# Three fp32r products of split halves in place of seven fp32 block products

## The chip, the cores and the metric

The kernel runs on one core of a Trainium2 chip. A core has five engines with an instruction stream each: TensorE (PE, matrix products; its weight loads are listed as PEld), VectorE (DVE), ScalarE (ACT), GpSimd (POOL) and SyncE (SP), which here issues every DMA. Each engine takes its instructions strictly in the order of its stream and waits where an operand isn't ready. SBUF is the working memory of 128 partitions; PSUM has eight banks into which PE writes its products. The metric is the device time in microseconds (us); lower is better. This text numbers the batch elements from 0 to 31 and calls the work of one turn of the outer loop a batch.

## The reference

The input x has 32 elements of 512 rows and 512 columns; adj is a 512 x 512 matrix of zeros and ones. Two layers follow each other, both with a residual and a layer normalisation:

```python
q, k, v = x @ Wq + bq, x @ Wk + bk, x @ Wv + bv        # 8 heads of 64 columns
scores = einsum('bihd,bjhd->bhij', q, k) / 8 + where(adj == 0, -1e9, 0)
x = layernorm(x + softmax(scores) @ v)
y = einsum('nm,bmd->bnd', adj, x)                      # aggregation
x = layernorm(x + y @ weight + bias)                   # convolution
```

The four products with a weight (three projections and the convolution) are 512 x 512 x 512 each, for every element.

## The kernel before

`fast_kernel` writes out the order of the work by hand; no scheduler moves an instruction. The tiles of one name and tag form a ring of a fixed number of buffers: a new tile takes the oldest buffer and waits until its last reader is done. All products go through one ring of eight PSUM banks.

Each of the four weight products is made by seven block products of 256 x 256 x 256 instead of eight (`FACTORS`, `block_product`, L365), in fp32, with sums of blocks of the weight made once (`sum_weights`) and sums of blocks of the transposed x (`combine_rows`, `sum_rows` on POOL) made for every element. The results are combined while they are taken out of the banks (`project`, L385 to L402, and `convolve`, L533 to L556). The weights stay in SBUF for the whole run.

The main loop runs over the elements b and two groups g of four heads. For a group, in this order:

- `attend` (L604, PE): exponentials times values, for two pairs of heads. `fold_squares` (L641, L643, DVE) and a DMA of parts sum the exponentials over the keys; `turn_out` (L621, DVE) transposes a pair's output and sends it to DRAM, from where `fetch_rows` (L629) brings it back as rows. `fetch_parts` (L655) brings the parts back.
- `scores` of the next group (L580, PE), sixteen banks, which DVE empties with the mask added (L582) and ACT exponentiates (L584). POOL adds the exponentials of the key blocks (`add_exponentials`, L595).
- for g = 0, `load_squares` of element b + 2 (L253): sixteen DMAs of 64 KB, in squares of 32, into the ring `xin` of four.
- the units of the slot (`units_of`). The first slot has the products for q and k and two for v of element b + 1, and between them the statistics and normalisations of b - 2 and b - 1 and `turn_over` (store of b - 2, then the load of x of element b into the same buffer). The second slot has the rest of v, the aggregation of b - 1 with adj (`aggregate`, L487, in fp32r, from a high and a low half of x that `split` makes: L455 on ACT, L459 on DVE), the four 32 x 32 transposes of element b + 2 (`turn_squares`, L350), and the convolution of b - 1, with the transposes between its products.

`scale_rows` (L675, ACT) and `add_rows` (L679, POOL) bring the attention's output into the residual. At the two ends of the run the order is written out separately: the first element is transposed on PE (`x_transpose`), and the last element's aggregation is done by rows (`aggregate_rows`) with the last normalisation in halves.

Of the kernel before, what the change touches and what calls it, by code (L numbers as in the profile page):

```python
# [23 lines left out]
FACTORS = {1: ("A11", "B11"), 2: ("A12", "B21"), 3: ("S4", "B22"), 4: ("A22", "T4"),  # L53
           5: ("S1", "T1"), 6: ("S2", "T2"), 7: ("S3", "T3")}
ORDER = (1, 5, 6, 7, 2, 3, 4)

A_AT = {"A11": 0, "A12": 1, "A21": 2, "S3": 2, "A22": 3, "S1": 4, "S2": 5, "S4": 6}
B_AT = {"B11": 0, "B21": 1, "B12": 2, "T3": 2, "B22": 3, "T1": 4, "T2": 5, "T4": 6}
# [147 lines left out]

@with_exitstack
def fast_kernel(ctx: ExitStack, tc, verdict, x, adj, Wq, bq, Wk, bk, Wv, bv, W1, b1, out):
# [6 lines left out]
    assert N == 512 and D == 512 and H * HD == D and B > 2  # L215
# [12 lines left out]


    X, IN = {}, {}  # L230
    half = N // 2

    def load(b):
        X[b] = work.tile([P, NB, D], FP, name="xT" if b == B - 1 > 1 else "xs", bufs=1 if b == B - 1 > 1 else 2)
        nc.sync.dma_start(X[b], x[b].rearrange("(c p) d -> p c d", p=P))

    def load_block(b, c, cols=slice(0, D)):

        if (b, c) not in IN:
            IN[b, c] = work.tile([P, D], FP, name="xin", bufs=XIN)  # L240
        nc.sync.dma_start(IN[b, c][:, cols], x[b, c * P:(c + 1) * P, cols])  # L241

    def load_squares(b):


        for d in range(DB):
            IN[b, d] = work.tile([P, N // SQ, SQ], FP, name="xin", bufs=XIN)
            place_squares(IN[b, d], x[b], d)
# [6 lines left out]
    def load_factors(w, name, t=None):  # L255
        if t is None:
            t = consts.tile([P, 7, 2, half], FP, name=name)
        for s in range(2):
            nc.sync.dma_start(t[:, 2 * s:2 * s + 2, :, :].rearrange("p a c f -> p (a c) f"),
                              w[:, s * half:(s + 1) * half].rearrange("(c p) f -> p c f", p=P))  # L260
        return t


    wq = consts.tile([P, 7, 2, half], FP, name="wq")

    def load_factor(name, r, c):
        nc.sync.dma_start(wq[:, B_AT[name], :, :], Wq[r * half:(r + 1) * half, c * half:(c + 1) * half].rearrange(
            "(c p) f -> p c f", p=P))

    for c in range(2):  # L270
        load_block(0, c, slice(0, half))
    load_factor("B11", 0, 0)
    for c in range(2):
        load_block(0, c, slice(half, D))
    for c in (2, 3):
        load_block(0, c)
    for name, r, c in (("B21", 1, 0), ("B12", 0, 1), ("B22", 1, 1)):
        load_factor(name, r, c)
# [11 lines left out]

# [11 lines left out]
    def look_for_low_half(c):  # L302

        kept = work.tile([P, N], FR, name="high")
# [3 lines left out]
        nc.vector.tensor_tensor(cut, squares, kept.bitcast(FP), op=ALU.not_equal)  # L308
        nc.vector.tensor_reduce(inexact[:, c:c + 1], cut, axis=AX.X, op=ALU.add)

# [3 lines left out]
    def sum_weights(w, n):  # L314

        b11, b21, b12, b22, t1, t2, t4 = (w[:, i, :, :] for i in range(7))
        nc.vector.tensor_sub(*((t1, b12, b11), (b12, b22, b12), (t2, b22, t1), (t4, b21, t2))[n])

    def combine(w, bias, which=range(4)):

        for n in which:
            sum_weights(w, n)
        width = bias.shape[1] // 2
        nc.vector.tensor_sub(bias[:, width:], bias[:, width:], bias[:, :width])

    def combine_rows(t, engine=nc.gpsimd, which=range(3)):

        a11, a12, a21, _, s1, s2, s4 = (t[:, i, :, :] for i in range(7))
        for n in which:
            engine.tensor_sub(*((s2, s1, a11), (a21, a11, a21), (s4, a12, s2))[n])  # L330

    def x_transpose(b, c, sides=(0, 1)):
# [636 lines left out]
```

## Time and profile before

| what | value |
|---|---|
| median of three runs | 2728.31 us (2727.42 to 2728.68) |
| span of the profiled execution | 2726.6 us; the page gives no other time of this execution |
| mean granted clock of TensorE | 0.999 |
| instructions | 36269 |
| DMA | 179.16 MB, mean 66 GB/s |

In the profile, busy time is the time in which an engine has at least one instruction running. A group of instructions is one source line (L365 is line 365 of the kernel), one engine and one shape, with how many there were, how long one took and what its engine had waited for. In a timeline each row has a start (in us from the start of the span), a length and a count of merged instructions; what stands in brackets is the idle time before it and its releaser. An fp32 product of TensorE stands in the records as two matmul instructions, an fp32r product as one. SPq is SyncE's queue of DMA issues; "to landing" is the time from an issue until the data are there.

### The profile page before, as it was taken

The page shows a single profiled execution, that of the slowest core. Times are in us where ns is not written, and L with a number is a line of the kernel's source. Part 1 is how long each engine was busy: PE and PEld are TensorE (multiplying, and loading weights), DVE is VectorE, ACT ScalarE, POOL GpSimd, SP SyncE. Part 2 cuts the span into 40 slices and gives each one's busy share as a digit, 9 for nine tenths or more (in the row PEclk, how much of TensorE's full clock was granted, in tenths as well). Part 3 has the DMA queues.
Part 4 walks back from the last instruction along what each step waited for, and adds up shares of the span by engine and source line. Part 5 has one row for each costly group of instructions (what it writes and reads, how often), then busy time and mean ns, then how long its engine had stood idle before and what let it go on. Part 6 is the DMA issues. An engine that isn't in the chain of part 4 may idle for free.

```text
span 2726.6 us, 36269 instructions
## 1 busy us (share of the span) xinstructions
PE 2715.0 (100%) x12328; PEld 1899.7 (70%) x12328; DVE 2106.5 (77%) x3476; ACT 1411.2 (52%) x2462; POOL 1916.0 (70%) x1221
## 2 busy tenths in 40 slices
PE   9999999999999999999999999999999999999998
PEld 6676676766767767667676676776767767667666
DVE  7878777777777787877878778777787777877778
ACT  3455464554544655446555465554554545546455
POOL 4776677766867668676676776777767776667776
PEclk9999999999999999999999999999999999999999
DMA  6213231233222332223322233221232212323121
GB/s 162 49 34 80 70 73 36 60 80 74 69 41 60 76 77 66 46 56 75 80 63 50 55 71 80 63 65 45 67 80 67 63 44 65 80 71 73 34 76 53
DMA packets 641166, 179.16 MB, mean 66 GB/s; under 512 B 586960, under 2 KB 591568, under 8 KB 640976
## 3 DMA queue, kind: packets, MB, share of 16 engines
q1 hardware_dynamic: 640976, 176.79, 27.6%
q8 instruction: 99, 1.62, 0.2%
q14 instruction: 91, 0.75, 0.1%
HBM read 108.01 MB, written 68.68 MB: 65 GB/s over the span
## 4 chain that ended last, share of the span: by engine, by line
PE 99%; DVE 0%; DMA 0%; POOL 0%; SPq 0%; ACT 0%; issue 0%; ACTq 0%
PE bank L365 57%; PE bank L580 17%; PE bank L604 16%; PE bank L487 9%; PE bank L519 0%; DMA xin<-in_x_dram 0%; DVE xT L550 0%; POOL xT L547 0%; DVE part L903 0%; SPq L241 0%; DVE shift L439 0%; PE bank L685 0%; ACT xT L444 0%; DVE stat L906 0%; PE bank L339 0%
## 5 line engine op out<-in xcount | busy, mean ns | idle before, releaser
L584 ACT ACTIVATE e<-e 128x1024 f32<-128x1024 f32 x512 | 524.5, 1052 | 570.4 <-DVE e L582 535.6
L595 POOL TENSOR_TENSOR es<-e 128x1024 f32<-128x1024 f32 x128 | 315.7, 2466 | 480.1 <-ACT e L584 480.1
L582 DVE SCALAR_TENSOR_TENSOR e<-gap,bank 128x512 f32<-128x512 uint8 x1024 | 618.0, 682 | 20.2 <-PE bank L580 20.2
L595 POOL TENSOR_TENSOR es<-es,e 128x1024 f32<-128x1024 f32 x256 | 618.6, 2417 | 20.1
L580 PE MATMUL bank<-q,k 64*128 64x512 f32 x2048 | 463.4, 598 | 0.0
L604 PE MATMUL bank<-e,v 128*64 128x512 f32 x2048 | 453.6, 595 | 0.0
L365 PE MATMUL bank<-wv,xT 128*128 128x256 f32 x1792 | 405.4, 381 | 0.0
L365 PE MATMUL bank<-xT,wk 128*128 128x256 f32 x1792 | 402.4, 379 | 0.0
L365 PE MATMUL bank<-xT,wq 128*128 128x256 f32 x1792 | 400.9, 381 | 0.6 <-ACT xT L341 0.5
L365 PE MATMUL bank<-w,yT 128*128 128x256 f32 x1792 | 392.3, 379 | 0.0
L365 PEld LDWEIGHTS bank<-wv,xT 128*128 128x128 f32 x1792 | 337.6, 190 | 70.1 <-DVE e L582 24.3
L365 PEld LDWEIGHTS bank<-xT,wq 128*128 128x128 f32 x1792 | 337.6, 190 | 69.2 <-DVE e L582 23.5
L580 PEld LDWEIGHTS bank<-q,k 64*128 64x128 f32 x2048 | 203.8, 186 | 258.1 <-issue 159.7
L365 PEld LDWEIGHTS bank<-w,yT 128*128 128x128 f32 x1792 | 340.0, 190 | 48.1 <-DVE e L582 0.8
L365 PEld LDWEIGHTS bank<-xT,wk 128*128 128x128 f32 x1792 | 340.5, 190 | 46.3
L675 ACT ACTIVATE rows<-rows,zero,inverse 128x64 f32<-128x64 f32 x1008 | 343.3, 429 | 1.9 <-DVE inverse L662 1.9
L604 PEld LDWEIGHTS bank<-e,v 128*64 128x64 f32 x2048 | 141.4, 137 | 277.1 <-issue 275.4
L584 ACT ACT_TABLE_LOAD x30 | 38.5, 1283 | 412.1 <-DVE e L582 412.1
L459 DVE TENSOR_TENSOR low<-xs,high 128x512 fp32r<-128x512 f32 x122 | 160.7, 1317 | 92.1 <-ACT high L455 92.1
L550 DVE TENSOR_TENSOR xs<-bank,xs 128x512 f32<-128x512 f32 x186 | 124.4, 683 | 96.2 <-PE bank L365 56.7
L444 ACT ACTIVATE xs<-xs,shift,rstd 128x512 f32<-128x512 f32 x248 | 181.8, 803 | 27.4 <-DVE shift L439 18.2
L490 ACT ACTIVATE yT<-bank 128x512 f32<-128x512 f32 x124 | 74.1, 598 | 185.0 <-PE bank L487 185.0
(122 smaller groups left out, 3050.8 us busy)
## 6 DMA issues: line engine op xcount, KB each, us to landing
turned<-attT SPq DMA_DIRECT2D x126, 256.0 KB, 2.1
rows<-turned SPq DMA_DIRECT2D x504, 64.0 KB, 2.5
xin<-in_x_dram SPq DMA_DIRECT2D x496, 64.0 KB, 2.4
xs<-in_x_dram SPq DMA_DIRECT2D x31, 1024.0 KB, 5.3
out_dram<-xs SPq DMA_DIRECT2D x31, 1024.0 KB, 4.4
part<-passed SPq DMA_DIRECT2D x256, 8.0 KB, 1.8
passed<-part SPq DMA_DIRECT2D x64, 32.0 KB, 1.5
wq<-in_L_gnn_Wq_dram SPq DMA_DIRECT2D x4, 256.0 KB, 5.9
```

Source lines behind the costliest of these rows:

```text
L365: nc.tensor.matmul(pm[:, r, :], left[:, d, r * P:(r + 1) * P], right[:, d, :], start=(d == 0), stop=(d == 1))
L444: nc.scalar.activation(row, row, AF.Identity, bias=SHIFT[t][:, slot:slot + 1], scale=RSTD[t][:, slot:slot + 1])
L459: nc.vector.tensor_sub(LOW[b, d], cols, HIGH[b, d].bitcast(FP))
L487: nc.tensor.matmul(pm.rearrange("p a n -> p (a n)"), part, adjT[:, n % NB, :], start=(n == 0), stop=(n == 2 * NB - 1))
L490: nc.scalar.activation(yt[:, d // 2:d // 2 + 3:2, d % 2, :], pm, AF.Copy)
L550: nc.vector.tensor_add(block, pm, block)
L580: nc.tensor.matmul(ps[s], keys[:, j * P:(j + 1) * P], queries, start=True, stop=True)
L582: nc.vector.scalar_tensor_tensor(e[:, s, :], gap[:, j, :], NEG * root, ps[s], op0=ALU.mult, op1=ALU.add)
L584: nc.scalar.activation(e, e, AF.Exp, scale=1.0 / root)
L595: nc.gpsimd.tensor_add(ES[b, hp], ES[b, hp] if j > 1 else E[b, hp, 0], E[b, hp, j])
L604: nc.tensor.matmul(po[s * HD:(s + 1) * HD, :], values, e[:, s, :], start=(j == 0), stop=(j == NB - 1))
L675: nc.scalar.activation(part, part, AF.Identity, bias=zero, scale=inverse[:, c, s:s + 1])
```

## The change

Every operand of the four weight products is split into two fp32r parts, and a product is made by three fp32r passes over 512 columns, in rows of 128: high x high, rest x rest (both scaled so that they add into one bank, `near`) and a mixed product (`both` x `both`) in a second bank, `far`. Two instructions take the pair out: ACT and DVE for q and k, DVE twice for v and for the convolution. A transposed x, and the aggregated y, is kept as three planes (`HIGH`, `REST`, `BOTH`) in one tile `factors` with a single buffer, which x of an element and y of another use in turn. The split of a plane is an ACT copy with a scale, a DVE operation on it and its source, and a POOL subtraction.

The planes of Wv and of the last weight stay in SBUF. Those of Wq and Wk don't: the first element makes them in eight chunks of 128 columns and stores them in DRAM, and every later element fetches them again, three chunks ahead, through SyncE's queue (24 DMAs of 256 KB for an element).

The order of units is new. The first slot holds the eight products for q and k, the second slot those for v, the aggregation, then the scores of the next element (`take_scores`), the convolution and, after all of it, the transposes and splits of x (`flips`). The low half for the aggregation moves from DVE to POOL. The launch and the end of the run are rewritten for the new products: the first weights are split as they arrive, and the last element's convolution is normalised and stored row block by row block.

```diff
-FACTORS = {1: ("A11", "B11"), 2: ("A12", "B21"), 3: ("S4", "B22"), 4: ("A22", "T4"),
-           5: ("S1", "T1"), 6: ("S2", "T2"), 7: ("S3", "T3")}
+EPSILON = 2.0 ** -12
+SHRINK = 1.0 - 2.0 ** -13
...
+    def split_high(high, a):
+        nc.scalar.activation(high, a, AF.Copy, scale=EPSILON * SHRINK)
+    def split_rest(rest, high, a):
+        nc.vector.scalar_tensor_tensor(rest, plain(high), -1.0 / EPSILON, a, op0=ALU.mult, op1=ALU.add)
+    def split_both(both, high, rest, engine=nc.gpsimd):
+        engine.tensor_sub(both, plain(high), plain(rest))
+    def split_weight(high, rest, both, w, temp):
+        nc.scalar.activation(high, w, AF.Copy, scale=SHRINK / EPSILON)
+        nc.scalar.activation(temp, w, AF.Copy, scale=SHRINK)
+        nc.vector.scalar_tensor_tensor(rest, w, 1.0 / EPSILON, plain(high), op0=ALU.mult, op1=ALU.subtract)
+        nc.gpsimd.tensor_sub(both, plain(rest), plain(temp))
+    def factors(name="factors"):
+        return work.tile([P, 3, DB, N], FR, name=name, tag="factors", bufs=1)
...
+    def turn_squares(b, d):
+        TURN[b, d] = work.tile([P, N], FP, name="turn", bufs=2)
+        nc.vector.transpose(TURN[b, d], IN[b, d].rearrange("p j f -> p (j f)"))
+    def split_x(b, d):
+        if d == 0:
+            XT[b] = factors()
+        high, rest, both = (XT[b][:, f, d, :] for f in range(3))
+        a = TURN.pop((b, d))
+        split_high(high, a)
+        split_rest(rest, high, a)
+        split_both(both, high, rest)
+    def flips(b):
+        return [(turn_squares, b, 0), (turn_squares, b, 1), (split_x, b, 0), (turn_squares, b, 2), (split_x, b, 1),
+                (turn_squares, b, 3), (split_x, b, 2), (split_x, b, 3)]
...
+    SEQUENCE = [(which, m) for m in range(DB) for which in "qk"]
+    AHEAD = 3
+    def chunks():
+        return [work.tile([P, DB, P], FR, name="stream", bufs=3 * AHEAD) for _ in range(3)]
+    def fetch_chunk(n):
+        b, (which, m) = n // len(SEQUENCE), SEQUENCE[n % len(SEQUENCE)]
+        CHUNK[b, which, m] = chunks()
+        for f, part in enumerate(CHUNK[b, which, m]):
+            nc.sync.dma_start(plain(part), KEPT[which, m, f])
+    def three_passes(near, far, left, right):
+        for f, pm in ((HIGH, near), (REST, near), (BOTH, far)):
+            for d in range(DB):
+                nc.tensor.matmul(pm, left(f, d), right(f, d), start=(f != REST and d == 0),
+                                 stop=(f != HIGH and d == DB - 1))
+    def project(b, which, m):
...
+        three_passes(near, far, lambda f, d: w[f][:, d, :], lambda f, d: xt[:, f, d, :])
+        if n + AHEAD >= len(SEQUENCE):
+            fetch_chunk(n + AHEAD)
+        t = store[b, m] = work.tile([P, N], FP, name=which, bufs=DB)
+        nc.scalar.activation(t, near, AF.Identity, bias=bias[:, m:m + 1], scale=1.0 + EPSILON)
+        nc.vector.tensor_add(t, far, t)
...
+    def convolve(b, r):
+        near, far = bank(N), bank(N)
+        three_passes(near, far, lambda f, d: yt[:, f, d, r * P:(r + 1) * P], lambda f, d: w1[:, f, d, :])
+        nc.vector.scalar_tensor_tensor(row, near, 1.0 + EPSILON, row, op0=ALU.mult, op1=ALU.add)
+        nc.vector.tensor_add(row, far, row)
...
+    def first_slot(b):
...
+        ready = [(turn_over, b)]
...
+            behind = [seen[:2], seen[2:] + old[:2], old[2:] + fresh[:2], ready + fresh[2:], young[:2], young[2:]]
+        behind += [scaled + added]
+        return [(add_up, b, 0)] + merge(projections(b + 1), behind)
+    def second_slot(b):
...
+        units = merge(values(b + 1), [splits[:1], splits[1:2], splits[2:3], splits[3:]])
+        units += [(add_up, b, 1)] + gathered[:2] + scaled[:1] + gathered[2:] + [(take_scores, b + 1, 0)]
...
+        units += merge(convolved, [scaled[1:] + added[:1], added[1:]])
+        return units + flips(b + 2)
...
+                if b + 2 < B:
+                    load_squares(b + 2)
+                units = first_slot(b)
+                run(units[:2])
+                run(later)
+                run(units[2:])
```

## The prediction

> **What bounds the kernel now.** I read the page's engine row first, then the chain of work in order of time over one batch (from 1302.53 us), then the timelines of VectorE and of SyncE's queue at that place, and last the rows in which something was late.
>
> ```profile
> PE 2715.0 (100%) x12328; PEld 1899.7 (70%) x12328; DVE 2106.5 (77%) x3476; ACT 1411.2 (52%) x2462; POOL 1916.0 (70%) x1221
> ```
> ```profile
> 1302.53 7.02 PE bank L604 x32
> 1309.55 7.14 PE bank L580 x32
> 1316.69 27.82 PE bank L365 x128
> ...
> 1364.05 3.74 PE bank L487 x16
> ...
> 1387.06 7.02 PE bank L604 x32
> ```
> TensorE (PE) never stands still, and a batch takes 1387.06 - 1302.53 = 84.53 us. An fp32 product is two passes in the records: 27.82 / 128 x 2 = 0.435 us for 256 columns. An fp32r pass over 512 columns is 3.74 / 16 = 0.234.
>
> ```profile
> 1310.64 9.66 DVE L582 SCALAR_TENSOR_TENSOR e<-gap,bank 128x512 f32<-128x512 uint8 x16 [0.33 <-PE bank L580]
> ```
> VectorE ends its folds and turnings with the two `attend`s (the last turning at 1310.31) and begins to empty the score banks 1.09 us after the scores began. Here is what happens when it is late, from the start of the run (VectorE and PE):
> ```profile
> 117.87 2.48 DVE L350 STREAM_TRANSPOSE xT<-xin 128x512 f32<-128x512 f32 x4
> 126.40 9.62 DVE L582 SCALAR_TENSOR_TENSOR e<-gap,bank 128x512 f32<-128x512 uint8 x16
> 124.10 8.31 PE L580 MATMUL bank<-q,k 64*128 64x512 f32 x32
> ```
> Four transposes stand straight before the folds, the emptying begins 2.30 us after the scores began, and the scores take 8.31 us where the steady batches' same row has 7.21.
>
> SyncE's queue in the same batch:
> ```profile
> 1309.84 2.61 SPq L629 DMA_DIRECT2D rows<-turned  x4
> 1312.55 1.99 SPq L655 DMA_DIRECT2D part<-passed  x4
> 1314.64 0.38 SPq L623 DMA_DIRECT2D turned<-attT  x1
> 1316.75 2.61 SPq L629 DMA_DIRECT2D rows<-turned  x4
> 1319.41 8.59 SPq L253 DMA_DIRECT2D xin<-in_x_dram  x16
> ```
> From the end of the second fold (1309.32) it is busy, in the order of the code (the passed parts first), until 1328.00: 18.7 us. Nothing on PE waits for it there today. A fetch from DRAM placed behind these would.
>
> Three prices (POOL and VectorE timelines; DMA issues and SyncE's waits; PE timeline at the run's first and late microseconds):
> ```profile
> 1367.22 2.80 POOL L595 TENSOR_TENSOR es<-e 128x1024 f32<-128x1024 f32 x1
> 1368.97 1.60 DVE L459 TENSOR_TENSOR low<-xs,high 128x512 fp32r<-128x512 f32 x1 [1.17 <-ACT high L455]
> ```
> ```profile
> turned<-attT SPq DMA_DIRECT2D x126, 256.0 KB, 2.1
> xs<-in_x_dram SPq DMA_DIRECT2D x31, 1024.0 KB, 5.3
> SPq L235 <- DMA out_dram<-xs: 118.3, 29, 5.8
> ```
> ```profile
> 1.06 3.36 PE L711 MATMUL bank<-attT 128*128 128x128 f32 x14 [1.06 <-DVE attT L708]
> 2683.95 1.03 PE L685 MATMUL bank<-ident,attT 128*128 128x128 f32 x8
> ```
> A VectorE instruction with two SBUF inputs waits for POOL's running one: L459 ended 0.55 us after L595 did. Alone such an instruction takes 0.65 to 0.7. 256 KB land in 2.1 us, and each further 256 KB in (5.3 - 2.1) / 3 = 1.07. A load of x waits 118.3 / 29 = 4.1 us for the store before it. A 128-column pass takes 0.24 us after the idle launch and 0.11 to 0.13 later.
>
> **The change, part by part.** t = 0 is the start of a batch's first `attend`.
>
> *PE work.* Per batch 112 fp32 products x 0.435 = 48.7 become 192 fp32r passes x 0.234 = 44.9: the batch would be 80.7 us. Over the run 3584 x 0.435 = 1559 become 6144 x 0.234 = 1438: -121. A project is 12 passes, 2.81 us.
>
> *Engine sums.* VectorE (65.0 us per batch) loses the block additions, the mixes and the low halves (372 + 168 + 161 + 26 us over the run, 23 per batch). It gains 8 additions for q and k, 8 evictions for v, 8 for the convolution, 4 rests of y at 0.65 and 4 rests of x at 0.65 to 1.3: 21 to 23. POOL (60.0) loses 20 and gains 4 low halves and 8 `split_both` at 1.27: 55. ScalarE (44.1) gains about 3.4. None exceeds 80.7, so no sum is the bound; order decides. POOL writing fp32r is in no row; VectorE's fp32r writes (0.68 at least) cost as its fp32 ones, so I take POOL's 1.27, and off the path up to twice that is covered.
>
> *VectorE before `attend`.* `flips` now stand behind the whole convolution, and `factors` has one buffer, so `split_x` waits for the convolution's last pass at t = 0. VectorE: last addition to 0.7, two transposes to 2.0, then `split_rest` (two SBUF inputs) among POOL's running work: exponential adds to 2.3, two residual adds, `split_both`, 1.27 each. With a wait at each rest they end at 2.9, 4.8, 6.75 and 8.65, the other two transposes in between. Never waiting, the last ends at 5.95. I take 8.65, by L459's median of 1.35. Then folds and turnings: second fold ends at 8.65 + 2.57 + 0.64 + 2.52 = 14.4 (today at 6.8), the last turning at 15.1. Banks: six scores run, the others wait for the two `attend` banks and the first evictions; project 0 needs the ninth eviction, 15.1 + 9 x 0.603 = 20.5, instead of 14.2. This alone is 6.4 us a batch.
>
> *The streamed weights.* Projects 0 to 2 find their chunks; project 3's is fetched by SyncE after project 0, in code order behind rows, parts and `load_squares`: 14.4 + 18.7 = 33.1, landed 2.1 later at 35.2. PE wants it at 14.2 + 3 x 2.81 = 22.6. The lag is 12.6 us and contains the 6.4; with VectorE never waiting on POOL, 9.9. Each chunk is 3 issues of 0.35; chunks 4 and 5 come in time within half a microsecond.
>
> *The gap.* PE then stands still for 35.2 - 28.9 = 6.3 us. Whether a slow clock follows is shown at the launch alone: 3.36 us at about half rate loses 1.6. Ends: 0 and 2.8 (project 3 wholly at half rate). I take the launch's 1.6.
> The Trainium skill, "TensorE: Matmul & The Clock Gate", Part 1, puts the array at half clock after an idle window of about 3.4 us until a busy one has passed; by it the term would be 1.7 to 3.4, which no row here can show, since PE has no such gap after the launch.
>
> *Chunk 7.* Its fetch stands behind `turn_over`. Project 3 ends at 39.6, chunk 6 is issued until 40.7, the store takes 0.4, the load waits 4.1 for it (45.2), chunk 7 goes out at 45.6. Alone its first part lands at 47.7 and PE wants it at 39.6 + 3 x 2.81 = 48.0: no cost. Behind the 1 MB load (lands at 50.5) it comes at 51.6: 3.6 us. I take 3.6, since both go out within half a microsecond on one queue; with the store itself behind chunk 6, 5.3.
> The Trainium skill, "DMA: Bandwidth & Descriptors", Queues, rings and completion order, says that each engine takes descriptors in ring order and that a completion lands after all earlier writes of that engine; by it the load comes first (3.6), and no row here shows two such transfers back to back.
>
> *Hidden.* The ScalarE chain (`scale_rows` of two pairs, 5.5 us, before project 7's eviction), the aggregation's splits and the second pair of `attend`s keep one to five microseconds of slack behind the late projects; without it they would be next.
>
> *Ends.* Launch: POOL must make 7 `split_both` (8.9 us, with VectorE's rests between them 13.4) before project 0 can close near 20; seven projects, scores and four values follow, 20 + 19.7 + 7.1 + 11.2 = 58 for the first `attend`, now 52: +6 (3 to 15), of which -3 is in the 121, so +9 beside it. Tail: `split_y` of four blocks before the last convolution, four `split_both` at 1.27: +5 (0 to 10).
>
> *Sum.* Span 2726.6 (the page gives the execution no other time; the median of the runs, 2728.3, is 1.7 longer, and that is added): 2728.3 - 121 + 9 + 5 = 2621. Lag per batch 12.6 + 1.6 + 3.6 = 17.8, in 29 batches with everything present: 516. Batch 0 about 13, batch 30 (no `load_squares`) 7: 20. Total 3157.
>
> **Rivals.** (A) VectorE is not late: the transposes and rests run while the convolution does. For: it idles a few microseconds there. Against: they stand behind it in the code. SyncE's fetch still comes at 6.8 + 18.7 + 2.1 = 27.6, 5.0 late: 2621 + 29 x 5 + 10 = 2776, with chunk 7 2880. (B) The other side: the streamed weights always arrive in time, and VectorE's work fits. Place: SyncE's fetch for project 3; it decides where the lag per batch falls under (2728 - 2621) / 29 = 3.7 us, so SyncE must get there 9 us sooner than counted. Price: 2621. Against: 18.7 us of issue are in the profile. (C) Only VectorE's 6.4 counts, the fetch is hidden: 2621 + 186 = 2807. (D) The stream is also short of bandwidth: each chunk 3 x 1.07 = 3.2 us against 2.81, five chunks, +2, and the late store, +1.7; with the gate's 2.8: 22.7 a batch, 3300.
>
> **How the numbers follow.** Forecast 0.66, own range 2621 + 29 x 9.9 + 12 = 2920 to 2621 + 29 x 20.7 + 35 = 3256; A 0.12; B 0.08; C 0.06; D 0.08. Low end 2790 takes in C and most of A; above 3270 lies D; about 0.2 stays out. A change under 0.2% can't be told from none: faster 0.07, same 0.01, slower 0.92.
>
> **What would show it.** PE busy near 85% with holes of 6 us before project 3 and 3 before project 7, released by the DMA stream; VectorE's first score eviction near 8 us after the scores began; L459-like `split_rest` near 1.3 us; fp32r passes of 0.234. It is wrong if the stream lands before SyncE's loads of squares end, if VectorE finishes its rests before t = 0, or if a batch takes under 84 us.

## The result and the profile after

The changed kernel takes 3345.45 us (median of four runs, 3338.51 to 3347.42) against 2728.0 for the kernel before on the same chip: a ratio of 1.2259 [1.2241, 1.2276], 617 us slower. The forecast was 3157 (2790 to 3270): right in direction, 188 us short, and outside its range. The profiled execution took 3345.0 us with a span of 3343.2 and a mean granted clock of 0.908 (before: 0.999).

The page of the changed kernel, its engine row, its row of granted clock over 40 slices, and its chain that ended last, by engine:
```profile
PE 2856.3 (85%) x11304; PEld 1870.7 (56%) x11304; DVE 2184.3 (65%) x3511; ACT 1566.9 (47%) x2586; POOL 1765.9 (53%) x1104
PEclk7888999889998899998899988999889998899999
...
PE 55%; DVE 16%; DMA 12%; SPq 10%; issue 4%; ACT 2%; POOL 1%; DVEq 0%; ACTq 0%; POOLq 0%
```
TensorE is busy for 85% of a longer span, and 38% of the chain now runs through VectorE, the DMAs and SyncE's queue (16, 12 and 10). Before, 99% of it was PE.

TensorE's timeline of one batch after the change (start, length, and in brackets the idle time before it):
```profile
1509.08 7.09 PE L556 MATMUL bank<-e,v 128*64 128x512 f32 x32
1516.09 2.85 PE L533 MATMUL bank<-q,k 64*128 64x512 f32 x12
1520.59 1.12 PE L533 MATMUL bank<-q,k 64*128 64x512 f32 x2 [1.65 <-DVE attT L570]
1523.65 6.96 PE L533 MATMUL bank<-q,k 64*128 64x512 f32 x18 [1.94 <-DVE attT L570]
1530.54 8.47 PE L376 MATMUL bank<-factors,stream 128*128 128x512 f32 x36
1545.13 12.94 PE L376 MATMUL bank<-factors,stream 128*128 128x512 f32 x48 [6.12 <-DMA stream<-kept_k]
1563.93 5.46 PE L376 MATMUL bank<-factors,stream 128*128 128x512 f32 x12 [5.87 <-ACT rows L627]
```
There are holes in three places: in the scores, before project 3 and before project 7. Where the 84.53 us batch before had none, this one lasts 104.63 us (1509.08 to 1613.71, the start of the next batch's first `attend`). The products beside the holes are slower too: project 7, alone behind a hole, takes 5.46 us for 12 passes, against 2.81 by the 0.234 of the prediction.

VectorE's timeline and then SyncE's queue at the same place:
```profile
1509.79 1.30 DVE L328 STREAM_TRANSPOSE turn<-xin 128x512 f32<-128x512 f32 x2
1511.27 1.76 DVE L296 SCALAR_TENSOR_TENSOR factors<-factors,turn 128x512 fp32r<-128x512 f32 x1 [0.18 <-ACT factors L293]
...
1517.37 1.23 DVE L592 STREAM_TRANSPOSE e<-es 128x1024 f32<-128x1024 f32 x1
...
1523.53 9.62 DVE L535 SCALAR_TENSOR_TENSOR e<-gap,bank 128x512 f32<-128x512 uint8 x16
```
```profile
1526.20 2.00 SPq L607 DMA_DIRECT2D part<-passed  x4
...
1530.40 2.61 SPq L578 DMA_DIRECT2D rows<-turned  x4
1533.05 8.60 SPq L232 DMA_DIRECT2D xin<-in_x_dram  x16
1541.75 1.38 SPq L370 DMA_DIRECT2D stream<-kept_k  x3
...
1547.21 3.05 SPq L370 DMA_DIRECT2D stream<-kept_q  x3
1550.35 0.39 SPq L456 DMA_DIRECT2D out_dram<-xs  x1
1557.46 0.38 SPq L217 DMA_DIRECT2D xs<-in_x_dram  x1
1557.94 1.82 SPq L370 DMA_DIRECT2D stream<-kept_k  x3
```
VectorE's transposes and splits of x (L328, L296) run beside `attend`, the folds begin behind them (1517.37), and the first score bank is emptied 7.4 us after the scores began (1523.53 against 1516.09). SyncE issues the sixteen loads of squares at 1533.05 and only then, at 1541.75, the chunk that project 3 needs from 1539.0 (1530.54 + 8.47). Chunk 6 goes out at 1547.21 and the store straight behind it at 1550.35. The last chunk, number 7, goes out at 1557.94, after a load of x that waited until 1557.46 for this store.

The chain in order of time shows what ended the wait before project 3 in that batch:
```profile
1541.16 0.49 SPq L232
1541.75 3.25 DMA stream<-kept_k
1545.13 9.33 PE bank L376 x32
```
A chunk is three parts of 256 KB. The first part of chunk 3 lands 3.25 us after its issue, and project 3 starts with it.

### The profile page after: what moved, and what is told of

Its sections match the earlier page's. It is cut to its first block, busy times and chain, and to the rows that moved or that the text cites. A ratio compares the mean times of both kernels' runs of the same rounds, so it can differ in the third digit from the quotient of the medians.

```text
span 3343.2 us, 36543 instructions
## 1 busy us (share of the span) xinstructions
PE 2856.3 (85%) x11304; PEld 1870.7 (56%) x11304; DVE 2184.3 (65%) x3511; ACT 1566.9 (47%) x2586; POOL 1765.9 (53%) x1104
## 4 chain that ended last, share of the span: by engine, by line
PE 55%; DVE 16%; DMA 12%; SPq 10%; issue 4%; ACT 2%; POOL 1%; DVEq 0%; ACTq 0%; POOLq 0%
PE bank L376 35%; DMA stream<-kept_k 7%; SPq L232 7%; PE bank L533 7%; PE bank L477 7%; PE bank L556 7%; DVE e L535 4%; DVE factors L296 4%; SPq L578 2%; DVE e L592 2%; DMA out_dram<-xs 2%; DVE part L595 2%; DMA turned<-attT 2%; DVE turn L328 1%; DVE attT L570 1%
## 5 line engine op out<-in xcount | busy, mean ns | idle before, releaser
L376 PE MATMUL bank<-factors,stream 128*128 128x512 f32 x3072 | 838.8, 437 | 319.6 <-DMA stream<-kept_k 309.4
L376 PEld LDWEIGHTS bank<-factors,stream 128*128 128x128 f32 x3072 | 652.1, 215 | 514.7 <-issue 176.2
L631 POOL TENSOR_TENSOR xs<-xs,rows 128x512 f32<-128x512 f32 x124 | 157.5, 1283 | 645.0 <-DMA stream<-kept_k 623.1
L299 POOL TENSOR_TENSOR factors<-factors 128x512 fp32r<-128x512 f32 x256 | 336.9, 1327 | 209.9 <-DVE factors L296 209.9
L376 PE MATMUL bank<-w,factors 128*128 128x512 f32 x1536 | 369.6, 399 | 4.7 <-ACT factors L293 4.0
L376 PE MATMUL bank<-wv,factors 128*128 128x512 f32 x1536 | 358.1, 392 | 0.0
L376 PEld LDWEIGHTS bank<-w,factors 128*128 128x128 f32 x1536 | 287.1, 189 | 96.1 <-ACT e L537 22.0
L376 PEld LDWEIGHTS bank<-wv,factors 128*128 128x128 f32 x1536 | 285.9, 188 | 84.1 <-issue 25.1
L449 POOL TENSOR_TENSOR halves<-xs,halves 128x512 fp32r<-128x512 f32 x120 | 154.5, 1288 | 163.6 <-ACT halves L445 163.6
L477 PE MATMUL bank<-adjT,halves 128*128 128x512 f32 x960 | 229.6, 396 | 0.0
```

The costliest lines, as they stand in the source:

```text
L299: engine.tensor_sub(both, plain(high), plain(rest))
L376: nc.tensor.matmul(pm, left(f, d), right(f, d), start=(f != REST and d == 0), stop=(f != HIGH and d == DB - 1))
L449: nc.gpsimd.tensor_sub(low, cols, plain(high))
L477: nc.tensor.matmul(pm, part, adjT[:, n % NB, :], start=(n == 0), stop=(n == 2 * NB - 1))
L631: nc.gpsimd.tensor_add(cols, cols, ROWS.pop((b, hp)))
```

## The experiments

The theory: the batch is longer by two separate things, VectorE's late start on the scores (about 7 us) and the order of SyncE's queue (the loads of squares ahead of chunk 3, the store and load ahead of chunk 7), and each hole is followed by slow-clock products. The rivals: the stream's bytes themselves are too many; a different engine (ScalarE's `scale_rows`, as the bracket before project 7 says) holds project 7; the slow clock is the larger part. The times of projects and of the second `attend` below are their starts, counted from the batch's first `attend`, as means over batches 5 to 25; "batch" is the mean length of batches 1 to 29:

| kernel | project 0 | project 3 | project 7 | second attend | batch (1 to 29) | whole, us |
|---|---|---|---|---|---|---|
| after | 21.73 | 36.19 | 54.01 | 58.67 | 102.94 | 3345.45 |
| squares late | 21.6 | 29.91 | 46.72 | 51.41 | 95.92 | 3130.48 |
| store and load late | 21.21 | 36.29 | 49.43 | 52.25 | 97.18 | 3171.65 |
| both late | 20.7 | 29.0 | 39.9 | 42.71 | 92.72 | 3039.99 |
| filler | 21.47 | 36.37 | 54.09 | 57.3 | 101.81 | 3317.62 |
| no stream | 21.61 | 29.91 | 40.79 | 43.6 | 88.19 | 2900.56 |
| order of the queue | 21.64 | 29.94 | 40.82 | 43.64 | 88.26 | 2902.14 |
| rest on POOL | 14.31 | 29.2 | 47.1 | 51.8 | 96.18 | 3144.3 |
| all four edits | 14.31 | 22.61 | 33.49 | 36.3 | 86.61 | 2833.53 |
| spread | 14.31 | 22.61 | 33.52 | 36.33 | 81.01 | 2666.48 |

**The squares moved.** The loads of squares of element b + 2 go behind the first slot instead of ahead of it.
```diff
-                if b + 2 < B:
-                    load_squares(b + 2)
                 units = first_slot(b)
...
                 run(units[2:])
+                if b + 2 < B:
+                    load_squares(b + 2)
```


> load_squares is issued after the first slot's units, nothing else moves. Theory (SyncE's order holds back the streamed weights): after the second pair's rows SyncE is free at about t = 24 in a batch, so chunk 3 is there before project 3 asks (t = 29.9) and the hole of 6.1 us before project 3 goes, with the 1.7 us by which projects 3 to 6 ran slow after it: 7.8 us a batch, 3345 - 30 x 7.8 = about 3110. The hole before project 7 stays. Rival (the stream is short of bandwidth, SyncE's place is not what counts): the hole stays at 5 us or more and the time is over 3280.

Measured: 3130.48 us, ratio 1.1477 [1.1444, 1.151], 3110 forecast. TensorE's timeline of this kernel:
```profile
1529.07 19.35 PE L376 MATMUL bank<-factors,stream 128*128 128x512 f32 x84
1553.44 5.33 PE L376 MATMUL bank<-factors,stream 128*128 128x512 f32 x12 [5.02 <-DMA stream<-kept_k]
```
Projects 0 to 6 run in one piece of 84 passes at 19.35 / 84 = 0.230 us each: the hole before project 3 is gone, and so are the slow passes behind it (project 3 to 6 take 10.65 us from first to last pass, 12.83 in the changed kernel). The second hole stays, now with the stream as its releaser. The squares ahead of chunk 3 cost 102.94 - 95.92 = 7.0 us a batch.

**The store and the load moved.** `turn_over` goes from behind project 3, where it stands ahead of the fetch of chunk 7, to behind project 7; `add_rows` follows it there, while `scale_rows` stays behind project 6.
```diff
...
-            behind = [seen[:2], seen[2:] + old[:2], old[2:] + fresh[:2], ready + fresh[2:], young[:2], young[2:]]
-        behind += [scaled + added]
+            behind = [seen[:2], seen[2:] + old[:2], old[2:] + fresh[:2], fresh[2:], young[:2], young[2:]]
+        behind += [scaled, ready + added]
```


> The store of b - 2 and the load of x (turn_over) are issued after project 7, add_rows after them. Theory (chunk 7's fetch waits on SyncE behind the load, which waits for the store): the hole of 5.9 us before project 7 goes and project 7 takes 2.8 instead of 5.4 us: 8.5 us a batch, about 3090. Rival 1 (project 7 waits for ScalarE's scale_rows, as its wait is labelled in the trace): the hole stays, over 3300. Rival 2 (the engines' share of DMA, 94% in that stretch, is what counts): the hole halves, about 3200.

Measured: 3171.65 us, ratio 1.1628 [1.1594, 1.1662]. TensorE's timeline:
```profile
1557.73 8.45 PE L376 MATMUL bank<-factors,stream 128*128 128x512 f32 x36
1571.83 15.98 PE L376 MATMUL bank<-factors,stream 128*128 128x512 f32 x60 [5.65 <-DMA stream<-kept_k]
```
Project 7 follows project 6 without a hole, though `scale_rows` stands where it stood: the bracket "ACT rows" before project 7 named the wrong releaser, and the second rival falls. Waiting for chunk 7 cost 102.94 - 97.18 = 5.8 us a batch. The forecast of 3090 was too low, since it took the hole and the slow project 7 from one batch (5.9 and 2.6 us). On average project 7 starts 17.82 - 13.14 = 4.7 us earlier behind project 3 and is 4.27 - 2.49 = 1.8 shorter from first to last pass. The second `attend` comes 58.67 - 52.25 = 6.4 us earlier, and 0.7 of that is lost again behind it.

**Both moved.** The two edits together.
```diff
...
-            behind = [seen[:2], seen[2:] + old[:2], old[2:] + fresh[:2], ready + fresh[2:], young[:2], young[2:]]
-        behind += [scaled + added]
+            behind = [seen[:2], seen[2:] + old[:2], old[2:] + fresh[:2], fresh[2:], young[:2], young[2:]]
+        behind += [scaled, ready + added]
...
-                if b + 2 < B:
-                    load_squares(b + 2)
...
                 run(units[2:])
+                if b + 2 < B:
+                    load_squares(b + 2)
```


> load_squares and turn_over both after the eight projects. Theory (two holds on SyncE's queue, nothing else, lie between this and the run without a stream): both holes go, a batch comes to 88 us as without the stream, about 2905; more than the sum of the two single gains (215 + 174 us, which would give 2957), because each hold hid a part of the other. Rival (the stream's bytes cost something by themselves): 91 us or more a batch, over 2985.

Measured: 3039.99 us, ratio 1.1144 [1.1121, 1.1166]: 10.2 us a batch gained, not 12.8, and 135 us above the forecast of 2905. The second `attend` comes as early as was hoped (42.71), but the batch is 92.72. SyncE's queue at the change of slots, and then what VectorE waited for in the whole run (total us, times, longest):
```profile
1513.36 0.39 SPq L456 DMA_DIRECT2D out_dram<-xs  x1
1518.88 0.38 SPq L217 DMA_DIRECT2D xs<-in_x_dram  x1
1519.32 10.48 SPq L232 DMA_DIRECT2D xin<-in_x_dram  x16
...
1530.43 0.38 SPq L600 DMA_DIRECT2D passed<-part  x1
```
```profile
DVE inverse L613 <- DMA part<-passed: 241.1, 31, 9.3
```
The queue's work has only been moved: the sums of the second pair of `attend`s can't be passed until 1530.43, and VectorE waits 241.1 / 31 = 7.8 us a batch for them, a row that the changed kernel doesn't have among its largest waits. The forecast left out whom the moved issues would stand in front of.

**A filler in the holes.** 22 products of adj with itself before project 3 and 20 before project 7, into a bank that is never read, keep TensorE busy in the holes.
```diff
+    def keep_busy(n):
+        pm = bank(N)
+        for _ in range(n):
+            nc.tensor.matmul(pm, adjT[:, 0, 0:P], adjT[:, 0, :], start=True, stop=True)
...
+        if 1 < b < B:
+            units[7:7] = [(keep_busy, 20)]
+            units[3:3] = [(keep_busy, 22)]
...
```


> 22 passes of adjT into a bank that nobody reads stand before project 3 and 20 before project 7, so that TensorE is busy in both holes; no transfer moves. Theory (after a hole TensorE runs at half clock for a few microseconds): projects 3 to 6 take 11.3 instead of 12.9 us and project 7 2.8 instead of 5.4: 4 us a batch, about 3220 although TensorE does 9.8 us more work in a batch. Rival (the projects are slow because their weights still arrive): no gain, 3345 or more.

Measured: 3317.62 us, ratio 1.2163 [1.2128, 1.2198]; the mean granted clock rises from 0.908 to 0.961. TensorE's timeline:
```profile
1526.51 5.19 PE L405 MATMUL bank<-adjT 128*128 128x512 f32 x22
1533.83 11.55 PE L376 MATMUL bank<-factors,stream 128*128 128x512 f32 x48 [2.13 <-DMA stream<-kept_k]
...
1552.44 4.57 PE L376 MATMUL bank<-factors,stream 128*128 128x512 f32 x12 [2.49 <-DMA stream<-kept_k]
```
From the first to the last pass, projects 3 to 6 take 11.16 us instead of 12.83, and project 7 takes 2.90 instead of 4.27: the slow passes do follow from the idle time. But project 7 starts at 54.09 as before (54.01), since its chunk comes no sooner: what the first filler saves, the second wait takes back. The batch gains 1.13 us, and the forecast of 3220 was too low: the slow clock after the first hole is real and off the path. The clock is not the larger part, and the third rival falls.

**No stream.** Elements from 1 on project q and k with the last three chunks that element 0 left in the buffers; the fetches of all other weights, and with them the right q and k of elements 1 to 31, are left out.
```diff
-        CHUNK[b, which, m] = chunks()
-        for f, part in enumerate(CHUNK[b, which, m]):
-            nc.sync.dma_start(plain(part), KEPT[which, m, f])
+        CHUNK[b, which, m] = CHUNK[0, "left", n % AHEAD]
...
+        if b == 0:
+            CHUNK[0, "left", n % AHEAD] = w
```


> No chunk is fetched after the first element: every later element's projections read the last three chunks again, so the projections of q and k of elements 1 to 31 use wrong weights; all else is done. Theory (stream and VectorE's lateness are two separate losses): both holes go and what is left over 80.7 us a batch is the scores' delay of about 7.3 us: a batch of 88 us, 3345 - 30 x 15 = about 2890. Rival (the batch is bound by VectorE, ScalarE or POOL once the stream is gone): 95 us a batch, about 3100. Rival on the other side (the scores' delay goes with the stream): 81 us, about 2690.

Measured: 2900.56 us, ratio 1.0634 [1.0603, 1.0665], 2890 forecast. All eight projects run in one piece, 96 passes in 22.05 us. Everything that has to do with fetching weights costs 102.94 - 88.19 = 14.75 us a batch. By the theory what is left of the loss, beside the launch and the end, is VectorE's; the last kernel below tests that. Bytes or order, this run alone can't say.

**The order of the queue alone.** The stream is back in full. The store goes behind project 4, the load behind project 5, and the squares into the second slot, ahead of the scores of the next element.
```diff
-        ready = [(turn_over, b)]
+        ready, then = [(store, b - 2)] if b > 1 else [], [(load, b)]
...
-            behind = [seen[:2], seen[2:] + old[:2], old[2:] + fresh[:2], ready + fresh[2:], young[:2], young[2:]]
+            behind = [seen[:2], seen[2:] + old[:2], old[2:] + fresh[:2], fresh[2:], young[:2] + ready, young[2:] + then]
...
-        units += [(add_up, b, 1)] + gathered[:2] + scaled[:1] + gathered[2:] + [(take_scores, b + 1, 0)]
+        units += [(add_up, b, 1)] + gathered[:2] + scaled[:1] + gathered[2:]
+        if b + 2 < B:
+            units += [(load_squares, b + 2)]
+        units += [(take_scores, b + 1, 0)]
...
-                if b + 2 < B:
-                    load_squares(b + 2)
```


> Only SyncE's order, in another way than in the run with both late: the store of b - 2 goes out after project 4, the load after project 5, and load_squares in the second slot before the scores. With both late a batch took 92.7 us, 4.5 more than without a stream. Theory (there the rows and parts of the second pair of attends stood behind store, load and squares, and ScalarE's scale_rows and VectorE's add_up waited for them): with these out of the way a batch takes 88 us as without the stream, about 2905. Rival (the stream's own bytes cost the 4.5 us): 92 us or more, about 3030.

Measured: 2902.14 us, ratio 1.0637 [1.0618, 1.0657], batch 88.26. TensorE's timeline:
```profile
1503.14 7.69 PE L533 MATMUL bank<-q,k 64*128 64x512 f32 x18 [1.94 <-DVE attT L570]
1510.76 22.09 PE L376 MATMUL bank<-factors,stream 128*128 128x512 f32 x96
```
With every weight fetched, this is the time of the kernel that fetches none (2902.14 against 2900.56). In this order the weights' 744 fetches of 256 KB cost 1.6 us in the whole run; their place in SyncE's queue cost 14.7 us a batch, 443 us in the run. The first rival falls. The Trainium skill ("DMA: Bandwidth & Descriptors", Issuing engines are not separate DMA queues) calls the sequencer's time to initiate a DMA usually small relative to the DMA itself. For one load of 64 KB here that is so (0.54 us of issue, 2.4 us to landing), but sixteen of them in a row hold SyncE for 8.60 us, and that time decided.

**The rests on POOL.** The rest of x is made by an ACT copy and a POOL subtraction instead of VectorE's instruction, and three transposes and three splits stand between the convolution's products and just behind them; the fourth of each follows the folds. The ring of transposed tiles has three buffers instead of two.
```diff
-        split_rest(rest, high, a)
+        nc.scalar.activation(both, plain(high), AF.Copy, scale=1.0 / EPSILON)
+        nc.gpsimd.tensor_sub(rest, a, plain(both))
...
-        units += merge(convolved, [scaled[1:] + added[:1], added[1:]])
-        return units + flips(b + 2)
+        turned = flips(b + 2)
+        units += merge(convolved, [scaled[1:] + added[:1], added[1:] + turned[:1], turned[1:2], turned[2:3]])
+        return units + turned[3:6]
...
+                if 0 < b < B - 1:
+                    run(flips(b + 1)[6:])
```


> The rests of x are made by POOL (from a descaled copy that ScalarE makes), and three of the four transposes stand between the convolution's products, the fourth behind the folds; the stream stays as it is. Theory (the scores wait because VectorE's rests, each behind a POOL instruction, stand before the folds): folds begin at 1 instead of 8.3 us after the first attend, the scores take 7.7 instead of 14.6 us, SyncE's chain comes 7 us earlier with them and the hole before project 3 stays at about 6: 7 us a batch, about 3135. Rival (POOL with four more subtractions of 1.27 us now makes project 0 wait): half of it is lost, over 3230.

Measured: 3144.3 us, ratio 1.1526 [1.1503, 1.1549], 3135 forecast. TensorE's timeline:
```profile
1526.64 7.36 PE L534 MATMUL bank<-q,k 64*128 64x512 f32 x32
...
1548.28 13.27 PE L377 MATMUL bank<-factors,stream 128*128 128x512 f32 x48 [5.88 <-DMA stream<-kept_k]
```
The 32 score passes run in one piece of 7.36 us, project 0 starts at 14.31 instead of 21.73, and the batch gains 6.8 us, although the hole before project 3 remains (5.88 us) and the one before project 7 too: SyncE's chain begins at the end of the folds, so it moved by as much as they did. VectorE and SyncE's order add up rather than hide each other.

The group of these rests in the changed kernel shows why VectorE was late (durations min/median/max in ns):
```profile
L296 DVE SCALAR_TENSOR_TENSOR factors<-factors,bank x132: 673/687/689, 5.9 to 3318.3; 128x512 fp32r<-128x512 f32 x132
L296 DVE SCALAR_TENSOR_TENSOR factors<-factors,turn x124: 676/1235/2086, 87.5 to 3165.0; 128x512 fp32r<-128x512 f32 x124
```
They are one instruction of the code: with one source in a PSUM bank it takes 687 ns, with both sources in SBUF 1235 by the median, and 676 at its fastest. The starts and ends in the trace say why. Of the 124 with both sources in SBUF, 93 begin while a POOL instruction runs, and they end 0.55 us after it (median); the 31 that begin beside none take 676 to 691 ns. Of the 132 with a PSUM source, 37 begin beside POOL as well, and none takes over 689. So POOL holds them up; no run took POOL away and left all else as it was. The Trainium skill ("SBUF — State Buffer", Who interferes with whom) says that a VectorE instruction with two SBUF inputs contends with a GpSimd instruction that reads SBUF; these rows agree.

**The launch.** The placing of adj's squares goes between the first projects, and the loads of the last weight, its bias and element 1's squares go behind the fifth.
```diff
-    for c in range(NB):
-        place_squares(adj_s[:, c, :, :], adj, c)
...
+    for c in range(NB):
+        run(first[c:c + 1])
+        place_squares(adj_s[:, c, :, :], adj, c)
+    run(first[4:5])
     nc.sync.dma_start(w1_raw, W1.rearrange("(c p) f -> p c f", p=P))
     b1_r = load_row(nc, consts, b1, "b1_r")
     load_squares(1)
...
-    run(first[:5])
```


> Only the launch: adj, the last weight and the squares of element 1 are issued between and behind the first five projects instead of before them. Theory (the stores of the first chunks stand on SyncE behind 23 us of loads, so the stream's buffers come free late and TensorE is idle from 34 to 61 us): the first attend begins at about 63 instead of 85 us, 3345 - 22 = 3323. Rival (ScalarE, VectorE and POOL need that time to split the weights): 80 us or later, 3340.

Measured: 3326.55 us, ratio 1.2194 [1.217, 1.2218], 3323 forecast; the first `attend` starts at 66.23 instead of 85.05. Those 18.8 us are the 18.9 that the run gains. The changed kernel's launch, SyncE's queue and then TensorE:
```profile
18.23 11.97 SPq L232 DMA_DIRECT2D xs<-in_adj_dram  x16
...
31.38 11.09 SPq L232 DMA_DIRECT2D xin<-in_x_dram  x16
42.98 1.32 SPq L361 DMA_DIRECT2D kept_k<-stream  x3
```
```profile
47.40 4.75 PE L533 MATMUL bank<-q,k 64*128 64x512 f32 x8 [13.23 <-ACT k L391]
```
The chunks of the first element must be stored before their buffers come free for the next ones; five of the eight stand behind 32 loads of squares, and TensorE stands still until they get through.

**All four.** Squares late, store and load late, rests on POOL and the launch, in one kernel; of the diff, lines of the first three.
```diff
...
-        split_rest(rest, high, a)
+        nc.scalar.activation(both, plain(high), AF.Copy, scale=1.0 / EPSILON)
+        nc.gpsimd.tensor_sub(rest, a, plain(both))
...
-            behind = [seen[:2], seen[2:] + old[:2], old[2:] + fresh[:2], ready + fresh[2:], young[:2], young[2:]]
-        behind += [scaled + added]
+            behind = [seen[:2], seen[2:] + old[:2], old[2:] + fresh[:2], fresh[2:], young[:2], young[2:]]
+        behind += [scaled, ready + added]
...
                 run(units[2:])
+                if b + 2 < B:
+                    load_squares(b + 2)
...
```


> All four moves together (squares late, turn_over late, rests on POOL with early transposes, launch). Theory (these are the whole loss, and beneath them the three passes are 3.8 us a batch shorter): a batch of 81.5 us, first attend at 63 us, the tail as it is: about 2675, faster than the kernel before by 2%. Rival (with the holes gone POOL's in-order work or VectorE's sum becomes the bound): 84 to 86 us a batch, 2740 to 2800.

Measured: 2833.53 us (four runs), ratio 1.0388 [1.0371, 1.0406], where 2675 was forecast. The first slot is as wanted: project 0 at 14.31, project 7 at 33.49, second `attend` at 36.3. The batch still takes 86.61. POOL's timeline:
```profile
1586.24 2.55 POOL L632 TENSOR_TENSOR xs<-xs,rows 128x512 f32<-128x512 f32 x2 [20.37 <-DMA xs<-in_x_dram]
```
This is the fault of "both moved" again: with the store, the load and the squares all behind project 7, the load of x comes late and POOL's residual additions wait 20.37 us for it, and VectorE waits for the parts (243.7 us in the run, 31 times). The spread kernel below has the same edits but for the order, and there this wait is 10.2 us in the run.

**Spread.** The order of the queue alone, with the rests on POOL and the launch; of the diff, lines that come in.
```diff
...
+        nc.scalar.activation(both, plain(high), AF.Copy, scale=1.0 / EPSILON)
+        nc.gpsimd.tensor_sub(rest, a, plain(both))
...
+    for c in range(NB):
+        run(first[c:c + 1])
+        place_squares(adj_s[:, c, :, :], adj, c)
...
+            behind = [seen[:2], seen[2:] + old[:2], old[2:] + fresh[:2], fresh[2:], young[:2] + ready, young[2:] + then]
...
+        if b + 2 < B:
+            units += [(load_squares, b + 2)]
+        units += [(take_scores, b + 1, 0)]
...
+        units += merge(convolved, [scaled[1:] + added[:1], added[1:] + turned[:1], turned[1:2], turned[2:3]])
...
```


> The same order with the rests on POOL, the early transposes and the launch of the run with all four moves. There a batch took 86.6 us; its second slot waited for rows, parts and the load of x. Theory (nothing else is left in a batch): 81 to 82 us, 66 + 78 + 29 x 81.5 + 69 + 102 = about 2680, faster than the kernel before by 1.8%. Rival (POOL's or ScalarE's order still holds the second slot): 84 us or more, 2755, slower than before.

Measured: 2666.48 us (2665.01 to 2668.65, five runs), ratio 0.9774 [0.976, 0.9787]: faster than both kernels, 2680 forecast. The page and TensorE's timeline:
```profile
PE 2612.6 (98%) x11304; PEld 1719.5 (65%) x11304; DVE 1995.5 (75%) x3387; ACT 1623.7 (61%) x2710; POOL 1911.3 (72%) x1228
```
```profile
1525.88 7.09 PE L557 MATMUL bank<-e,v 128*64 128x512 f32 x32
1532.90 7.36 PE L534 MATMUL bank<-q,k 64*128 64x512 f32 x32
```
The batch is 81.01 us, 0.3 above the 80.7 of PE work that the prediction counted. The products of the change do save 3.6 us a batch (84.6 - 81.0); what kept them from it was where the work around them stands.

## Why the prediction was right and wrong

VectorE's lateness, SyncE's queue ahead of chunk 3 and both holes came where the prediction had put them. Five terms of the sum failed. The slow clock behind the second hole was put at nothing, without a reason: it costs 1.8 us a batch, 52 in the run. The load's wait for the store ahead of chunk 7 was priced from a kernel without a stream: 1.4 us a batch too little, 41 in the run. The landing of chunk 3 was 1.0 us too short, 29 in the run. The launch left SyncE's queue out of its sum (27 us), and the end left out two waits of TensorE (16).

**PE work, -121: held.** 96 passes in 22.05 to 22.09 us are 0.230 each against the 0.234 taken, and a batch almost without waits is 81.01 us against 80.7.

**VectorE before `attend`: held, slightly short.** The second fold ends at t = 13.9 in the batch shown (forecast 14.4), the emptying begins at 14.5 (15.1), project 0 starts at 21.73 on average (20.5). From the emptying to project 0 it is 7.0 us in that batch, where the step had 9 x 0.603 = 5.4; the granted clock in the scores (0.76, below) lies there, and no run prices it. The price was 6.4 us a batch; taking the cause away gave 6.8 in the changed kernel, and 88.26 - 81.01 = 7.25 between the two kernels with the better queue. Rival A is thereby refuted.

**Chunk 3 behind SyncE's chain: held.** The loads of squares end at t = 32.6 in the batch shown (forecast 33.1), and project 3 starts at 36.19 on average (35.2). The term missed is the landing: 3.25 us in the chain, taken at 2.1. The 2.1 is that of `turned`, a store of 256 KB, and a chunk is three fetches of 256 KB; which of the two differences counts was not tried. The loads of squares just ahead are not it: the first part of chunk 3 lands 2.9 us after its issue (median) in the changed and in the squares-late kernel alike. Rival B's condition, that the queue reaches the fetch sooner, is what the spread order fulfils.

**The gap's slow clock, 1.6: it exists, but the step put it in the wrong place.** The changed kernel's granted clock, DMA share and GB/s (last three columns; each row begins with its stretch and length) for the scores, projects 3 to 6, and the hole with project 7:
```profile
1516.09:1530.54 14.45, 10.86 (x34) 5.76 (x32) 14.38 (x22) 5.38 (x6) 6.36 (x5) 0.76 0.24 59
1545.13:1558.07 12.94, 12.94 (x48) 10.24 (x48) 3.87 (x9) 5.27 (x9) 0.00 (x0) 0.85 0.79 280
1558.07:1569.32 11.25, 5.39 (x13) 3.80 (x13) 0.69 (x1) 6.48 (x18) 2.51 (x2) 0.70 0.94 335
```
Behind project 3 the loss is 12.83 - 10.65 = 2.2 us, but the wait for chunk 7 absorbs it (the filler run). A second stretch, in project 7, costs 4.27 - 2.49 = 1.8 us that the step did not count at all, though the prediction had a hole of 3.6 us before it, and that one is on the path: where the filler shortens project 7 by 1.4 us, the batch gains 1.13. The first row shows a third stretch, in the scores.

**Chunk 7 behind `turn_over`, 3.6: the term that was mis-sized.** From the start of project 3 to that of project 7 it is 54.01 - 36.19 = 17.8 us, where the prediction had 51.6 - 35.2 = 16.4. Its way behind the load was sized rightly: from its issue to its first product, chunk 7 takes 1563.93 - 1557.94 = 6.0 us in the batch shown, and 51.6 - 45.6 = 6.0 in the forecast. What was too short is the load's wait for the store. SyncE's row for it in the changed kernel, and then in the squares-late kernel:
```profile
SPq L217 <- DMA out_dram<-xs: 157.4, 29, 6.6
SPq L217 <- DMA out_dram<-xs: 111.9, 29, 5.0
```
157.4 / 29 = 5.4 us, taken at 4.1 from the kernel before. In the changed kernel the store goes out 0.1 us behind chunk 6 and lands after 5.8 us (the page's median). Where it goes out 2.9 us behind chunk 6 (squares late, median), it lands after 4.2 and the wait is 111.9 / 29 = 3.9; without a stream the page has 4.2 as well. This points at the chunk straight ahead of the store; it is read from these kernels and not tried by itself. The prediction had named the case ("with the store itself behind chunk 6, 5.3") and taken the other; in its terms the hole is 3.6 + 1.4 = 5.0. With its slow clock it cost 5.8 us a batch in the end (second experiment). Rival D came nearest in time (3300), in part by luck: its late store (1.7 us a batch) is near the 1.4 measured, but its shortage of bandwidth (2 us a batch) is refuted as a cause of its own, since in another order the same bytes cost next to nothing.

**Hidden work: held.** ScalarE's chain did not become the bound in the changed kernel. The label before project 7 said otherwise, and the second experiment refutes the label.

**Launch, first `attend` at 58: failed.** It came at 85.05. The step summed POOL's, VectorE's and PE's work and left out SyncE's: the 23 us of loads ahead of most stores of the first chunks, 12 of them for adj. Moving them gave back 18.9; the first `attend` then stands at 66.23, so that the rest of the step (58) was also some 8 short.

**End, +5: failed.** From the last element's first `attend` it is 101.5 us (83.7 before), so +18. The trace shows two waits there that no steady batch has: 4.70 us in the scores, whose banks wait for VectorE's turning (its fold waits 4.00 us for POOL's sum of the exponentials there), and 3.98 before the last convolution for ACT's first split, with slow passes behind it. No run tested this; the spread kernel has the same 101.5.

**The sum.** Of the 188 us: launch +27, batch 0 +12 (86.9 against 75.2), batches 1 to 29 +129 (102.94 against 98.5), batch 30 +8 (84.4 against 72.4 before, less 2.8 for its three cheaper products, plus 7: 76.6), end +16 (101.5 against the 85.9 that its +5 makes of 83.7 with the cheaper products); together 192, which agrees within 4. The 4.4 per batch are +1.0 at project 3, +1.4 from there to project 7, +1.8 of slow clock in project 7 and 0.2 behind it. The upper bound of its own range, 3256, allowed a lag of 20.7 us a batch, with the late store and the slowest first gap in it, and 102.94 - 80.7 = 22.2 was measured: 29 x 1.5 = 45 of the 89 us beyond it. A second slow stretch was in no bound. The rest lies in the launch, batches 0 and 30 and the end.

## What to carry to other kernels

In this kernel an added transfer was priced by its place in the issuing queue and not by its bytes: the same 24 fetches an element cost 14.7 us or next to nothing. So list what is issued ahead of a transfer, and what it then stands in front of. When issues are moved, spread them over stretches in which nobody waits for the queue; moved as a block behind project 7, they cost 138 and 167 us more than spread (3039.99 - 2902.14, 2833.53 - 2666.48). In the sum, each hole of 5 to 6 us needs a term of its own for the slow clock behind it. The releaser in a bracket is a hint: before believing it, leave the named work where it is and move the other suspect, as the second experiment did.

## What was not expected of the hardware

- A wait of 5 to 6 us on TensorE slows what follows: 48 passes take 12.83 us instead of 10.65 (granted clock 0.85 over them), and 12 passes 4.27 instead of 2.49 (0.70 with the hole). Products into an unread bank during the wait bring 11.16 and 2.90. The Trainium skill ("TensorE: Matmul & The Clock Gate", Part 1) puts the array at half clock after an idle window of about 3.4 us until a busy one; losses of 2.2 and 1.8 us agree with that. In the scores two waits of 1.65 and 1.94 us, with 1.12 us of products between them, come with a granted clock of 0.76 over 14.45 us, so that one unbroken wait of that length isn't needed.
- Transfers on one queue hold each other up. A 1 MB store landed in 4.2 us where 2.9 us lay between it and the chunk ahead, and in 5.8 straight behind a chunk (page medians of the squares-late and the changed kernel). The 256 KB parts of k's chunks took 5.4 us with the store and the load among them and 3.8 with both moved late; in the stretch of the hole with project 7 the DMA engines were busy for 0.94 of their time at 335 GB/s.
